# Loads over all partitions, and products of a zero block at the start, in a cross-attention and FFN kernel

## The chip, the cores and the metric

The kernel runs on one core of a Trainium2 chip, all in float32 (some operands in the fp32r form of it). The metric is the device time of one execution in microseconds, as the median of several runs. Beside these runs there is one profiled execution, from which all durations below are read.

## The reference

The input is x, 16 batches of 128 rows by 1024, and a context of the same shape. One layer of cross-attention is followed by a feed-forward product, each with a residual:

```python
x = x + xattn(layernorm(x), ctx, ctx, Wq, bq, Wk, bk, Wv, bv, Wo, bo)
x = x + ffn(layernorm(x), kernel, scale)
# xattn: Q = q @ Wq + bq (1024 -> 1024, 32 heads of 32)
#        K, V = ctx @ Wk + bk, ctx @ Wv + bv (1024 -> 256, 8 heads of 32; 4 query heads share one)
#        softmax(Q K^T / sqrt(32)) V per head, then @ Wo + bo
# ffn:   scale * concat(x[:819], -4 * x[819:]) @ kernel  (kernel: zeros and ones, 1024 x 1024)
```

## The kernel before

The batches go in groups of two (GB = 2), eight groups in all. For each group the kernel transposes the context, makes K and V, normalizes and transposes x, makes Q, runs the attention of each batch and head group, then the output projection and the feed-forward product. The large products (q, k, o, f) are done from the second group on in a form with seven half-size products in place of eight; sums of weight blocks that this needs are made early on (by GpSimd for Wq and Wo, in `combine`), stored in DRAM, and read again.

The order of the instructions is written out by hand. A `Stream` holds generators of matrix work in a queue, and events that fire at given times after a point ("later(us, fn)"). Every engine takes its instructions in the order in which this recording issues them. Thus a vector instruction that waits for a load also holds up what stands behind it on VectorE.

Weights come through a ring of eight tiles named `piece` (512 KB each, `fetch`, L243); the SP queue issues a new piece as soon as PE has released an old one. Nearly all transfers are issued on SP's queue (SPq in the profile), in order.

The context of a batch is loaded by `load_ctx` (L166) into a tile of 128 partitions x [4 blocks t][8 chunks c][32]. VectorE's 32x32 block transposes (`turn_ctx`, L445) then make the transposed context cT of it. For that the tile must have, on partition 32k + r, the rows 32t + r and the columns 256k to 256k + 255. Before the change each of the four DMAs of such a load fills one quarter of the partitions (fixed k, all t):

```python
src = key_value[b].rearrange("(t r) (k c f) -> k r t (c f)", r=32, k=NB, c=NC)
for k in range(NB):
    dst = c_t[k * 32 : (k + 1) * 32].rearrange("r t c f -> r t (c f)")
```

Wv and Wk are loaded once at the start in the same permuted order of rows, by `load_by_quadrants` (L175), as twelve and eight DMAs on three queues (ACT, GpSimd, SP). In the later groups normalized rows of x and of the input of the feed-forward product take the same way: `through_dram` stores a row tile in DRAM (L409) and reads it back in the block layout (L406, tiles `turn_x` and `turn_f`), for block transposes on VectorE (L471 and L983). The reading back must wait until the store has landed.

At the start the order is: context of batch 0, Wv, context of batch 1, Wk, then x of batches 0 and 1 (L183), the broadcast bias bo_b (L217), six pieces of Wq, the context of batches 2 and 3, two more pieces, eight half-size parts of Wo. PE starts with v for batch 0 and batch 1 (L418), then k, then the transposes of x (L434) and the products q of the first group.

Of the kernel before, what the change touches and what calls it, by code (L numbers as in the profile page):

```python
# [9 lines left out]
FP = mybir.dt.float32  # L10
# [8 lines left out]
P = 128  # L19
# [76 lines left out]
def kernel(  # L96
# [16 lines left out]
    nc = tc.nc  # L113
# [7 lines left out]
    NC = D // P  # L121
# [10 lines left out]
    const = ctx.enter_context(tc.tile_pool(name="const", bufs=1))  # L132
# [3 lines left out]
    ps_mm = ctx.enter_context(tc.tile_pool(name="ps_mm", bufs=2, space=PSUM))  # L136
# [6 lines left out]
    wk_sb = const.tile([P, NC, KV], FP, name="wk_sb")  # L143
    wv_sb = const.tile([P, NC, KV], FP, name="wv_sb")
# [13 lines left out]

    NB = P // 32

    def load_ctx(b, queues=(nc.sync,)):
        c_t = work.tile([P, NB, NC, 32], FP, tag="ctx", name=f"ctx{b}", bufs=2)
        src = key_value[b].rearrange("(t r) (k c f) -> k r t (c f)", r=32, k=NB, c=NC)
        for k in range(NB):
            dst = c_t[k * 32 : (k + 1) * 32].rearrange("r t c f -> r t (c f)")
            queues[k % len(queues)].dma_start(out=dst, in_=src[k])  # L166
        cs[b] = c_t

    def load_by_quadrants(dst, w, queues, *cuts):

        src = w.rearrange("(k c f) n -> k f c n", k=NB, f=32)
        n = 0
        for lo, hi in zip((0,) + cuts, cuts + (NC,)):
            for k in range(NB):
                queues[n % len(queues)].dma_start(  # L175
                    out=dst[k * 32 : (k + 1) * 32, lo:hi], in_=src[k][:, lo:hi]
                )
                n += 1

    def load_x(b, tag="row"):  # L180

        x_t = work.tile([P, D], FP, tag=tag, name=f"xn{b}", bufs=2)
        nc.sync.dma_start(out=x_t, in_=x[b])  # L183
        xns[b] = x_t
        if tag == "turn":
            turning.add(f"xn{b}")
# [11 lines left out]

    three = (nc.sync, nc.scalar, nc.gpsimd)
    load_ctx(0, three)
    load_by_quadrants(wv_sb, Wv, (nc.scalar, nc.gpsimd, nc.sync), 2, 4)
    load_ctx(1, three)
    load_by_quadrants(wk_sb, Wk, (nc.scalar, nc.gpsimd, nc.sync), 4)
    load_x(0)
    load_x(1)
    ident = const.tile([P, P], FP, name="ident")
    make_identity(nc, ident)
    minus_half = const.tile([P, 1], FP, name="minus_half")  # L210
# [183 lines left out]
    def through_dram(row, name, store, back, turn, then, tag="turn"):  # L394

        there = dram.tile([P, D], FP, name=f"dram_{name}")

        def load():
            bufs = 2 if tag == "turn" else TB
            c_t = work.tile([P, NB, NC, 32], FP, tag=tag, name=f"turn_{name}", bufs=bufs)  # L400
            if tag == "turn":
                turning.add(name)
            src = there.rearrange("(t r) (k n) -> k r t n", r=32, k=NB)
            for k in range(NB):
                dst = c_t[k * 32 : (k + 1) * 32].rearrange("r t c f -> r t (c f)")
                nc.sync.dma_start(out=dst, in_=src[k])  # L406
            stream.later(turn - back, lambda: then(c_t))

        stream.later(store, lambda: nc.sync.dma_start(out=there, in_=row) and None)  # L409
        stream.later(back, lambda: stream.when(lambda: tag != "turn" or len(turning) < 2, load))  # L410
# [718 lines left out]
    with tc.manual_schedule():  # L1129
# [17 lines left out]
        for j in range(GB):  # L1147
            load_ctx(GB + j)
# [83 lines left out]
        for grp in range(NGRP):  # L1232
# [39 lines left out]
            if not more:  # L1272
                for q in range(2 * NA):
                    b, a = grp * GB + q % GB, q // GB
                    start = stream.now
# [5 lines left out]
            for q in range(2 * NA):  # L1281
                b, a = grp * GB + q % GB, q // GB
                start = stream.now
# [64 lines left out]
```

## Time and profile before

| | |
|---|---|
| median of 3 runs | 770.59 us (770.08 to 770.86) |
| profiled execution, its own time | 765.46 us |
| span of the profile | 763.7 us |
| PE busy (TensorE's matrix instructions) | 746.6 us, 98% |
| DVE / ACT / POOL busy | 541.5 / 380.2 / 303.2 us |
| bytes moved by DMA | 203.36 MB, mean 266 GB/s |
| median time to landing, ctx loads on SP | 7.2 us, 128 KB each |
| median time to landing, turn_f and turn_x loads | 4.5 and 6.2 us, 128 KB each |

PE is TensorE's matrix instructions, PEld its weight loads, DVE VectorE, ACT ScalarE, POOL GpSimd; SPq is the queue of transfers that SyncE issues. Each float32 product shows as two matrix instructions in the profile. In rows of windows the columns are the window and its length, busy time of PE, PEld, DVE, ACT and POOL with the number of instructions, the granted clock of TensorE (1.00 is full), the mean busy share of the sixteen DMA engines and their rate in GB/s. An execution's own time is longer than its span by what lies around it, here 1.8 us.

### The profile page before, as it was taken

What the parts mean: (1) busy time and instruction counts of PE and PEld (TensorE: products, weight loads), DVE (VectorE), ACT (ScalarE), POOL (GpSimd) and SP (SyncE); (2) the same over time, 40 slices, a digit from 0 to 9 for tenths busy, and PEclk for the clock granted to TensorE, in tenths of its full rate; (3) what the DMA queues carried; (4) which work ended last, traced back from release to release, by engine and by line L of the source; (5) the groups of instructions that cost most, each with busy time, mean ns of one, the idle gap of its engine ahead of it and who ended that gap; (6) DMA issues with size and microseconds to landing.
All of it is one profiled execution on the core that took longest, in us unless ns stands there. A gap on an engine that the chain in (4) does not pass through costs nothing.

```text
span 763.7 us, 14898 instructions
## 1 busy us (share of the span) xinstructions
PE 746.6 (98%) x5232; PEld 563.4 (74%) x5232; DVE 541.5 (71%) x961; ACT 380.2 (50%) x1397; POOL 303.2 (40%) x356
## 2 busy tenths in 40 slices
PE   4999999999999999999999999999999999999997
PEld 3888884699747996489855998469984699546466
DVE  1456888977787667677676687865778766769586
ACT  0245764444735455344643447434464455568363
POOL 4069830342740146401652226322274113108582
PEclk9999999999999999999999999999999999999999
DMA  9989999989499895999779995899948988752912
GB/s 229 311 319 295 372 372 412 324 272 347 158 326 267 283 319 173 316 261 294 253 244 294 297 292 201 282 314 272 316 165 297 274 274 266 240 194 83 286 45 110
DMA packets 104314, 203.36 MB, mean 266 GB/s; under 512 B 8960, under 2 KB 58432, under 8 KB 104240
## 3 DMA queue, kind: packets, MB, share of 16 engines
q1 hardware_dynamic: 102480, 200.31, 81.8%
q10 hardware_dynamic: 1248, 1.11, 0.7%
q0 software_dynamic: 512, 0.99, 0.6%
q8 instruction: 41, 0.67, 0.4%
q14 instruction: 33, 0.27, 0.1%
HBM read 170.40 MB, written 31.98 MB: 265 GB/s over the span
## 4 chain that ended last, share of the span: by engine, by line
PE 90%; DVE 7%; DMA 2%; issue 1%; ACT 0%; SPq 0%; DVEq 0%
PE q_u L558 13%; PE o_u L862 12%; PE f_u L1017 7%; PE tpp L802 7%; PE q_v L558 7%; PE o_v L862 7%; PE k_u L558 5%; PE sc L769 4%; PE av L811 4%; PE q L418 4%; PE f_v L1017 3%; PE q_c L558 3%; PE k_v L558 3%; PE o_c L862 3%; PE f_c L1017 2%; PE k L418 2%
## 5 line engine op out<-in xcount | busy, mean ns | idle before, releaser
L785 ACT ACTIVATE p<-sc,negm 128x128 f32<-128x128 f32 x512 | 181.2, 370 | 147.3 <-DVE negm L781 73.1
L781 DVE TENSOR_REDUCE negm<-sc 128x4 f32<-128x512 f32 x128 | 86.9, 682 | 72.5 <-PE sc L769 72.5
L356 POOL CAST wide<-wf_sb 128x512 fp32r<-128x512 int8 x154 | 109.2, 749 | 64.0 <-PE f_u L1017 62.7
L804 ACT COPY pt<-tpp 128x512 f32<-128x512 f32 x128 | 75.1, 595 | 96.9 <-PE tpp L802 96.3
L797 DVE TENSOR_TENSOR p<-p,inv 128x512 f32<-128x512 f32 x128 | 103.4, 808 | 4.4
L785 ACT ACTIVATION_READ_ACCUMULATOR p<-sc,negm 128x1 f32 x512 | 106.3, 208 | 0.0
L196 POOL TENSOR_TENSOR x<-x,bo_b 128x256 f32<-128x256 f32 x64 | 50.3, 806 | 87.6 <-DMA x<-in_x_dram 74.9
L558 PE MATMUL q_u<-t,piece 128*128 128x128 f32 x672 | 81.3, 275 | 0.0
L558 PEld LDWEIGHTS q_u<-t,piece 128*128 128x128 f32 x672 | 78.1, 192 | 0.2 <-issue 0.2
L802 PE MATMUL tpp<-ident,p 128*128 128x128 f32 x512 | 75.9, 273 | 1.6 <-DVE p L797 1.6
L802 PEld LDWEIGHTS tpp<-ident,p 128*128 128x128 f32 x512 | 61.3, 141 | 20.1 <-issue 13.6
L862 PE MATMUL o_v<-piece,s 128*128 128x512 f32 x128 | 60.6, 601 | 0.2 <-DVE x L876 0.2
L862 PE MATMUL o_u<-piece,s 128*128 128x512 f32 x128 | 59.7, 597 | 0.5 <-DVE x L876 0.5
L862 PE MATMUL o_u<-piece,yT 128*128 128x512 f32 x128 | 58.6, 599 | 0.0
L819 ACT ACTIVATE yT<-av,bvT 128x512 f32<-128x512 f32 x32 | 22.0, 688 | 60.3 <-PE av L811 60.3
L769 PEld LDWEIGHTS sc<-kv,qT 32*128 32x128 f32 x1024 | 31.5, 186 | 25.7 <-issue 25.7
L374 POOL TENSOR_TENSOR rs_f<-ve_f,minus_half 128x1 f32<-128x1 f32 x16 | 9.5, 595 | 96.1 <-DVE ve_f L372 83.0
L961 POOL TENSOR_TENSOR s<-turn_f,turn_f 128x512 f32<-128x512 f32 x7 | 8.9, 1277 | 97.3 <-DVE turn_f L983 71.0
L354 ACT CAST wide<-wf_sb 128x512 fp32r<-128x512 int8 x70 | 43.2, 633 | 3.3 <-PE f_u L1017 3.0
L862 PEld LDWEIGHTS o_u<-piece,yT 128*128 128x128 f32 x128 | 23.5, 190 | 28.4 <-issue 26.7
L862 PEld LDWEIGHTS o_u<-piece,s 128*128 128x128 f32 x128 | 23.0, 190 | 27.6 <-issue 22.7
L862 PEld LDWEIGHTS o_v<-piece,s 128*128 128x128 f32 x128 | 22.4, 190 | 23.3 <-issue 18.9
(155 smaller groups left out, 1493.0 us busy)
## 6 DMA issues: line engine op xcount, KB each, us to landing
piece<-o SPq DMA_DIRECT2D x64, 512.0 KB, 4.8
piece<-q SPq DMA_DIRECT2D x56, 512.0 KB, 7.1
piece<-in_L_xattn_Wq_dram SPq DMA_DIRECT2D x50, 512.0 KB, 8.0
piece<-in_L_xattn_Wo_dram SPq DMA_DIRECT2D x48, 512.0 KB, 7.1
piece<-kv SPq DMA_DIRECT2D x18, 512.0 KB, 6.9
xn<-in_x_dram SPq DMA_DIRECT2D x16, 512.0 KB, 4.6
x<-in_x_dram SPq DMA_DIRECT2D x16, 512.0 KB, 5.1
ctx<-in_ctx_dram SPq DMA_DIRECT2D x60, 128.0 KB, 7.2
```

The source lines that it names most:

```text
L196: lambda cut=cut: nc.gpsimd.tensor_add(x_t[:, cut], x_t[:, cut], bo_b[:, cut]) and None,
L356: nc.gpsimd.tensor_copy(t, wf_sb[:, FFN[name], c])
L418: nc.tensor.matmul(mm, lhsT=lhsT, rhs=rhs, start=k == 0, stop=k == n - 1)
L558: nc.tensor.matmul(mm if part is None else mm[:, part], lhsT=lhsT, rhs=rhs, start=start and n == k == 0, stop=k == len(some) - 1, skip_gro ...
L769: nc.tensor.matmul(tiles[i][:, g], lhsT=qT[rows, g], rhs=kT[rows], start=True, stop=True,)
L781: nc.vector.tensor_reduce(negm, tile_, AX.X, ALU.max, negate=True)
L785: nc.scalar.activation(p[:, g], tile_[:, g], AF.Exp, bias=negm[:, g : g + 1], accum_out=total[:, g : g + 1],)
L797: nc.vector.tensor_mul(p, p, inv.unsqueeze(2).to_broadcast([P, NG, S]))
L802: nc.tensor.transpose(tp[:, g], p[:, g], ident)
L804: nc.scalar.copy(pt, tp)
L862: nc.tensor.matmul(mm, lhsT=lhsT[:, 2 * k + c], rhs=w[:, c], start=start and k == c == 0, stop=k == c == 1, skip_group_check=True,)
L1017: nc.tensor.matmul(mm, lhsT=part[:, c], rhs=w, start=start and c == n == 0, stop=c == HC - 1 and n == 1, skip_group_check=True,)
```

## The change

Three things change. First, each block load (context, and the readings back in `through_dram`) is cut the other way: each of its four DMAs now fills all 128 partitions for one t, with one packet of 1 KB per partition, as before 128 packets in all. Second, Wv and Wk are loaded with eight DMAs each, each over all partitions for one chunk c; the first loads are issued on two queues (SP and ACT) in place of three. Third, VectorE fills a 128x128 tile with zeros at the start, and TensorE multiplies it by itself nine times into a PSUM tile that nobody reads.

```diff
+    def blocks_in(dst, src, queues=(nc.sync,)):
+        src = src.rearrange("(t r) (k n) -> t k r n", r=32, k=NB)
+        for t in range(NB):
+            queues[t % len(queues)].dma_start(
+                out=dst[:, t].rearrange("p c f -> p (c f)"), in_=src[t]
+            )
+
     def load_ctx(b, queues=(nc.sync,)):
         c_t = work.tile([P, NB, NC, 32], FP, tag="ctx", name=f"ctx{b}", bufs=2)
-        src = key_value[b].rearrange("(t r) (k c f) -> k r t (c f)", r=32, k=NB, c=NC)
-        for k in range(NB):
-            dst = c_t[k * 32 : (k + 1) * 32].rearrange("r t c f -> r t (c f)")
-            queues[k % len(queues)].dma_start(out=dst, in_=src[k])
+        blocks_in(c_t, key_value[b], queues)
         cs[b] = c_t
 
-    def load_by_quadrants(dst, w, queues, *cuts):
-
-        src = w.rearrange("(k c f) n -> k f c n", k=NB, f=32)
...
+    def load_rows(dst, w, queues):
+
+        src = w.rearrange("(k c f) n -> c k f n", k=NB, f=32)
+        for c in range(NC):
+            queues[c % len(queues)].dma_start(
+                out=dst[:, c], in_=src[c]
+            )
...
-    three = (nc.sync, nc.scalar, nc.gpsimd)
-    load_ctx(0, three)
-    load_by_quadrants(wv_sb, Wv, (nc.scalar, nc.gpsimd, nc.sync), 2, 4)
-    load_ctx(1, three)
-    load_by_quadrants(wk_sb, Wk, (nc.scalar, nc.gpsimd, nc.sync), 4)
+    two = (nc.sync, nc.scalar)
+    load_ctx(0, two)
+    load_rows(wv_sb, Wv, two)
+    load_ctx(1, two)
+    load_rows(wk_sb, Wk, two)
     load_x(0)
     load_x(1)
+    blank = const.tile([P, P], FP, name="blank")
+    nc.vector.memset(blank, 0.0)
+    warm = ps_mm.tile([P, P], FP, tag="mm", name="warm")
+    for _ in range(9):
+        nc.tensor.matmul(warm, lhsT=blank, rhs=blank, start=True, stop=True)
...
-            src = there.rearrange("(t r) (k n) -> k r t n", r=32, k=NB)
-            for k in range(NB):
-                dst = c_t[k * 32 : (k + 1) * 32].rearrange("r t c f -> r t (c f)")
-                nc.sync.dma_start(out=dst, in_=src[k])
+            blocks_in(c_t, there)
             stream.later(turn - back, lambda: then(c_t))
```

Nothing else moves in the order of any engine's instructions.

More of the change, by code (lines that the diff above doesn't have):

```diff
@@ L159 @@
     NB = P // 32
+    def blocks_in(dst, src, queues=(nc.sync,)):
[4 more added lines that the diff above has]
+            )
     def load_ctx(b, queues=(nc.sync,)):
         c_t = work.tile([P, NB, NC, 32], FP, tag="ctx", name=f"ctx{b}", bufs=2)
-        src = key_value[b].rearrange("(t r) (k c f) -> k r t (c f)", r=32, k=NB, c=NC)
-        for k in range(NB):
-            dst = c_t[k * 32 : (k + 1) * 32].rearrange("r t c f -> r t (c f)")
-            queues[k % len(queues)].dma_start(out=dst, in_=src[k])
+        blocks_in(c_t, key_value[b], queues)
         cs[b] = c_t
-    def load_by_quadrants(dst, w, queues, *cuts):
-        src = w.rearrange("(k c f) n -> k f c n", k=NB, f=32)
-        n = 0
-        for lo, hi in zip((0,) + cuts, cuts + (NC,)):
-            for k in range(NB):
[L175 to L178, printed above, removed]
+    def load_rows(dst, w, queues):
[4 more added lines that the diff above has]
+            )
     def load_x(b, tag="row"):
@@ L402, in load @@
                 turning.add(name)
-            src = there.rearrange("(t r) (k n) -> k r t n", r=32, k=NB)
-            for k in range(NB):
-                dst = c_t[k * 32 : (k + 1) * 32].rearrange("r t c f -> r t (c f)")
-                nc.sync.dma_start(out=dst, in_=src[k])
+            blocks_in(c_t, there)
             stream.later(turn - back, lambda: then(c_t))
```

## The prediction

> **What bounds the kernel now.** I read the page first, then PE's waits, the chain of waits, the windows and the issue timeline.
>
> ```profile
> span 763.7 us, 14898 instructions
> PE 746.6 (98%) x5232; PEld 563.4 (74%) x5232; DVE 541.5 (71%) x961; ACT 380.2 (50%) x1397; POOL 303.2 (40%) x356
> ```
>
> TensorE is busy for all but 17.1 us of the span. Where the rest lies, the waits of PE say (us in total, times, longest):
>
> ```profile
> PE v L418 <- DMA wv_sb<-in_L_xattn_Wv_dram: 7.6, 2, 7.1
> PE v L418 <- DVE cT L445: 2.1, 1, 2.1
> PE tpp L802 <- DVE p L797: 1.6, 3, 0.8
> ```
>
> Only the first two concern loads: 9.7 us, all ahead of 15.88 us. After that PE never waits for a transfer. The chain of waits has the start in order of time (start, us):
>
> ```profile
> 2.12 5.02 DMA wv_sb<-in_L_xattn_Wv_dram
> 7.16 7.83 DMA ctx<-in_ctx_dram
> ...
> 15.88 3.72 PE v L418 x16
> 19.60 6.92 PE k L418 x32
> ```
>
> The windows give the rate of transfers in their last column, the DMA engines' share before it:
>
> ```profile
> 4.00:6.00 2.00, 0.00 (x0) 0.00 (x0) 0.03 (x1) 0.00 (x0) 1.82 (x4) 1.00 1.06 241
> 12.00:14.00 2.00, 1.79 (x8) 1.20 (x6) 0.00 (x0) 0.00 (x0) 0.00 (x0) 1.00 1.19 207
> 22.00:24.00 2.00, 2.00 (x11) 1.74 (x10) 1.49 (x3) 0.48 (x1) 0.48 (x1) 1.00 1.10 348
> 114.60:133.70 19.10, 19.10 (x83) 9.53 (x83) 16.75 (x34) 8.36 (x36) 1.20 (x2) 1.00 1.04 412
> ```
>
> Loads into 32 partitions (the first two rows) hold all engines busy, yet move 207 to 241 GB/s; transfers over 128 partitions, many with the same 1 KB packets, move 348, and 412 in the best stretch: 412/16 = 25.8 GB/s for one DMA engine. Last, one later group on SP's issue queue, and the vector transposes that use what it loaded:
>
> ```profile
> 419.53 8.24 SPq L166 DMA_DIRECT2D ctx<-in_ctx_dram  x8
> 430.66 0.38 SPq L409 DMA_DIRECT2D dram_f<-x2n  x1
> 437.41 2.62 SPq L406 DMA_DIRECT2D turn_f<-dram_f  x4
> 443.90 1.75 SPq L406 DMA_DIRECT2D turn_f<-dram_f  x4
> ```
> ```profile
> 452.48 1.31 DVE L983 STREAM_TRANSPOSE turn_f<-turn_f 128x512 f32<-128x512 f32 x2 [0.42 <-DMA turn_f<-dram_f]
> ```
>
> VectorE already waits 0.42 us for the second turn_f load: that transfer is just in time. It lands at about 452.4.
>
> **The changed loads.** Each load of a 512 KB block still is four DMAs of 128 KB, 128 packets of 1 KB. The destination gets 128 rows, but the source, written as (k r), has 4 as its outermost count and 32 inside it; before, both sides had 32 outermost, and every other bulk transfer 128. No row of before shows a transfer with fewer than 16 entries outermost, so its price is bounded from both sides. The good end is the 348 GB/s row: all engines at work, and every partition written. The bad end is that the engines are dealt out by the outermost count: 4 of 16, at worst the same four each time, so 4 x 25.8 = 103 GB/s. I take the bad end. The 32-row loads with a share of 1.06 to 1.19 show that 32 entries occupy all engines. Four entries cannot be dealt to sixteen engines without cutting them, and source and destination no longer have a common count of 16 or more in their first place. The nearest row for the speed of one engine is then the 412 row.
>
> The Trainium skill has a rule on this, on the page "DMA: Bandwidth & Descriptors", section "Why a DMA increments its semaphore by 16 and not by 1": a DMA gets the largest number of engines up to 16 that divides the slowest dimension of both patterns, and on the queues of SP and ACT these are the lowest-numbered. By it 128 and 4 give four engines, always the same; by the opposite case of 16 engines the sum would be rival B's. No row of before shows it.
>
> On those four engines a 128 KB block load puts 32 KB on each, and so does a 512 KB transfer over sixteen. At 25.8 GB/s either takes 1.27 us of them.
>
> *Start.* 24 loads x 1.27 = 30.5 us, begun at 2.1: the last of wk lands at 32.6. In the trace k ran from 19.4 with no wait. v for batch 1 needs ctx1, the 16th load (2.1 + 20.3 = 22.4), and hides in wk's landing. After the last wk come four instructions of k's first half (0.9) and its second half (3.46, half of 6.92): k ends at 37.0 rather than 26.5. The two xn loads queue behind wk on SP and land at 33.9 and 35.2; the normalization took 3.3 us for the first (20.05 to 23.33) and 3.1 for the second: 40.3. Then the transposes of x end near 42.6, where they ended at 28.6: **+14 us**.
>
> What is late next is the stream of transfers behind. bo_b and six pieces land by 44.0, ctx2 and ctx3 (8 x 1.27) by 54.2, two pieces and Wo's eight half-size parts by 61.8. In the trace GpSimd had the first of these parts at 41.2 and the rest by 43.9, so its sums start about 18 us later. It then is 96% busy (18.34 of 19.10 us) until 79, and the sums of Wq that it makes are stored, reloaded (issued 83.6 to 90.3) and used by PE from 89.4: nearly no slack. ctx4 and ctx5 add 8 x (1.27 - 0.60) = 5.4 us ahead of those stores (0.60 is 128 KB at 218 GB/s, a rate between the first two windows' rows). 18 + 5.4 is 23.4; with 1.6 us for the queue behind, **+25 us** by there, the 14 included. Bounds: 13, if the later stream is hidden, and 35, if an engine makes only 348/16 = 21.8 GB/s.
>
> *Each later group (91 us).* Between 419.5 and the use of the second turn_f stand 16 block loads and 8 other transfers: 24 x 1.27 = 30.5 us on the four engines. With the backlog at 419.5 (four transfers, 5 us) and 1.5 us to land: 456.5 rather than 452.4. If SP also drains while it waits for dram_f, the store that each turn_f load must follow (2 to 3 us, twice), it is 461. So VectorE stands still for 4 to 9 us; behind it in its queue are the maxima and the divisions of the softmax, and PE's transposes of p wait for these. Their slack (PE takes p at 358.7 that was divided by 353.3) covers some. I take 5 us for each of six groups: **+30 us**. Bounds: 0, and 11 where 65 transfers' worth (41 of 512 KB, 24 block loads) at 21.8 GB/s need 98 us rather than 91 and the wait for dram_f drains the queue as well.
>
> **The other edits.** GpSimd issues no first loads any more: its first block (about 5 us at 0.55 to 0.72 each) is off the path. ACT and SP issue twelve each at 0.31 to 0.45 us, less than the 1.27 us each takes to move; behind ACT's stands the table load (1.28 us), needed only by k's end. The memset costs about 0.22 us (the row of ident's) on a VectorE that first works at 5.97. Nine products are 18 instructions (each of v's 16 products shows as two of its 32); at twice the 111.6 ns spacing of 128x128 instructions (3.57/32) they take 4.0 us, about 1.2 to 5.2, and PE was idle until 7.13. If that cover were gone, they would cost at most those 4.0 us.
>
> What can they bring? v's first instruction took 767 ns and the next ones 634, with starts 0.43 us apart, against 379 and 0.216 later; the clock column shows 1.00 all through. Ten such starts are 2.1 us, and in before the wait for ctx1 (15.88) swallowed them. I take 0, with -2.1 as the other end where PE's first products set the pace.
>
> The skill's "TensorE: Matmul & The Clock Gate", Part 1, says that the array runs at half rate until some 3.4 us of activity and falls back after an idle window as long. The slow starts ended about 4.8 us after the first, near that. By it products that end at 5.2 ahead of a v later than 8.6 are forgotten: 0 again.
>
> **Sum.** 25 + 30 = 55 us. The profiled execution took 765.46 us (1.8 around the span), 5.1 under the median; added to the median of 770.59 this is 826 us.
>
> **Rivals.**
> - A, only the start suffers: four engines, but the slack in each group covers the delay. For it: SP waits mostly for PE to free pieces. Against: the 0.42 us row. 770.6 + 13 to 25 = 784 to 796.
> - B, faster: the loads run on all engines. 3 MB at 348 GB/s is 9.0 us rather than some 14 at 207 to 262, so ctx1 lands near 10 and v for batch 1 starts 4 to 5 us before 15.88; the products add up to 2.1. 764 to 767 us. It decides where the first loads move over about 262 GB/s, the most that a window of before's start shows. Against it: the outermost 4.
> - C, no difference: the loads get no faster, or what they gain is lost behind xn (20.05): 770.6 within 1.5 us.
>
> **How the numbers follow.** Forecast 0.57, A 0.25, B 0.15, C 0.03. Changes under 0.2% (1.5 us) are what a measurement here cannot tell from none. Slower 0.82, faster 0.15, same 0.03. The range takes A's low end with a small start, 776, and goes to 890, the high bounds (35 + 66 = 101, so 872) with some room for one engine slower than 21.8 GB/s; B and C stay outside.
>
> **What would show it.** Right: about 100 GB/s in the windows from 2 to 32 us, k ending near 37, later waits of DVE for turn_f by several us, and waits of PE for p or for pieces in each group. Wrong: 300 GB/s or more in the first windows with v for batch 1 before 12 us (B), or a late start followed by groups of 91 us (A).

## The result, and the profile after

The changed kernel takes 902.83 us (median of 6 runs, 899.81 to 906.37) against 769.76 us before (6 runs): the ratio is 1.1735, 95% interval 1.1701 to 1.1768. The profiled execution took 901.46 us, its span is 899.7 us, 136.0 us longer than the one before. The forecast was 826 us with a range up to 890: slower, as forecast, but by 133.1 us in place of 55.

The page of the changed kernel, first rows:

```profile
span 899.7 us, 14920 instructions
PE 787.7 (88%) x5250; PEld 591.5 (66%) x5250; DVE 543.5 (60%) x962; ACT 381.1 (42%) x1397; POOL 295.9 (33%) x347
```

PE's idle time grew from 17.1 to 112.0 us (899.7 - 787.7), that is by 94.9; its busy time grew by 41.1 us for 18 more instructions. The two make up the 136.0. The busy part is explained further down; the idle part is named by PE's waits (us in total, times, longest), of which the five largest are:

```profile
PE q_u L561 <- DMA piece<-q: 50.2, 10, 7.9
PE q_v L561 <- DMA piece<-q: 15.3, 8, 3.7
PE v L421 <- DVE cT L448: 12.8, 2, 7.5
PE o_v L865 <- DVE x L879: 8.7, 3, 4.9
PE k L421 <- DMA wk_sb<-in_L_xattn_Wk_dram: 4.9, 3, 3.8
```

Before, PE waited for loads at the start only. Now it waits 65.5 us for pieces of Wq, loads that the change does not touch: they queue behind the block loads. VectorE waits for the block loads themselves, and SP for the store that each turn_f must follow. First both lines as they were before, then after:

```profile
DVE turn_f L983 <- DMA turn_f<-dram_f: 6.3, 5, 2.9
...
SPq L406 <- DMA dram_f<-x2n: 45.5, 12, 7.1
```
```profile
DVE turn_f L986 <- DMA turn_f<-dram_f: 105.4, 14, 13.4
...
SPq L164 <- DMA dram_f<-x2n: 86.9, 13, 10.0
```

The windows at the start answer to those of before that showed a share of 1.06 to 1.19 (second to last column; the last is GB/s):

```profile
10.00:12.00 2.00, 0.00 (x0) 0.00 (x0) 0.07 (x1) 0.00 (x0) 0.00 (x0) 1.00 0.27 96
20.00:22.00 2.00, 2.00 (x4) 0.90 (x4) 0.00 (x0) 0.00 (x0) 0.00 (x0) 1.00 0.27 96
```

A share of 0.27 is about 4 of 16 engines. The windows from 10 to 30 us all read 0.27 and 96 or 97 GB/s; 96.5 GB/s / 4 = 24.1 GB/s for one engine, and a 128 KB load takes 131072 B / 96.5 GB/s = 1.36 us. The share stays there for 20 us with several loads under way on two queues, so all of them run on the same four engines. PE's timeline has the start (start, us, instructions, in brackets the idle time and who ended it):

```profile
43.73 6.05 PE L421 MATMUL k<-cT,wk_sb 128*128 128x256 f32 x18 [3.82 <-DMA wk_sb<-in_L_xattn_Wk_dram]
...
51.88 8.37 PE L421 MATMUL q<-xT,piece 128*128 128x256 f32 x38
```

q of the first group starts at 51.88 instead of 28.6. And one later group, SP's queue and then VectorE, at the place where the prediction showed it for before:

```profile
403.77 12.17 SPq L164 DMA_DIRECT2D ctx<-in_ctx_dram  x8
...
418.40 0.38 SPq L412 DMA_DIRECT2D dram_f<-x2n  x1
...
429.34 2.22 SPq L164 DMA_DIRECT2D turn_f<-dram_f  x4
431.66 0.46 SPq L412 DMA_DIRECT2D dram_f<-x2n  x1
432.22 1.17 SPq L249 DMA_DIRECT2D piece<-q  x2
439.54 2.21 SPq L164 DMA_DIRECT2D turn_f<-dram_f  x4
```
```profile
438.70 0.71 DVE L986 STREAM_TRANSPOSE turn_f<-turn_f 128x512 f32<-128x512 f32 x1 [11.93 <-DMA turn_f<-dram_f]
...
449.57 1.30 DVE L986 STREAM_TRANSPOSE turn_f<-turn_f 128x512 f32<-128x512 f32 x2 [5.79 <-DMA turn_f<-dram_f]
```

From the issue of a store of dram_f to the load that must follow it there are 10.9 us and 7.9 us; before, these gaps were 6.8 us (430.66 to 437.41) and 3.8 us (440.13 to 443.90). VectorE stands still 11.93 and 5.79 us for the two loads, where it stood 0.42 us before. Meanwhile the two pieces issued at 432.22 wait behind the block loads, and PE stands still too (PE's timeline):

```profile
440.89 2.90 PE L561 MATMUL q_u<-t,piece 128*128 128x128 f32 x12 [7.88 <-DMA piece<-q]
```

To split the loss by place, q_c, the first product of the halved form in each group, gives a clock that can be read in every run. In the summary of that tile (first and last start) its first instruction is at 85.2 us before and 112.9 after, its last at 626.5 and 750.9, and 137.2 and 148.8 us follow to the end. So the start costs 27.7, the six spans between 96.7 (16.1 each), and the end 11.6 us: 136.0.

### The profile page after: what moved, and what is told of

It is laid out like the page before. It is cut to its first block, busy times and chain, and to the rows that moved or that the text cites. A ratio compares the mean times of both kernels' runs of the same rounds, so it can differ in the third digit from the quotient of the medians.

```text
span 899.7 us, 14920 instructions
## 1 busy us (share of the span) xinstructions
PE 787.7 (88%) x5250; PEld 591.5 (66%) x5250; DVE 543.5 (60%) x962; ACT 381.1 (42%) x1397; POOL 295.9 (33%) x347
## 4 chain that ended last, share of the span: by engine, by line
PE 51%; DMA 30%; DVE 8%; SPq 7%; POOL 2%; issue 1%; DVEq 0%; ACT 0%; POOLq 0%
DMA dram_f<-x2n 12%; PE o_u L865 8%; SPq L164 6%; PE f_u L1020 6%; PE q_u L561 5%; PE o_v L865 5%; DMA piece<-q 5%; PE tpp L805 4%; PE q_v L561 4%; PE k_u L561 4%; PE sc L772 3%; PE av L814 3%; PE f_v L1020 3%; DMA turn_f<-dram_f 2%; DMA wv_sb<-in_L_xattn_Wv_dram 2%; PE k_v L561 2%
## 5 line engine op out<-in xcount | busy, mean ns | idle before, releaser
L561 PE MATMUL q_u<-t,piece 128*128 128x128 f32 x672 | 95.1, 301 | 50.2 <-DMA piece<-q 50.2
L561 PEld LDWEIGHTS q_u<-t,piece 128*128 128x128 f32 x672 | 90.5, 216 | 52.0 <-DVE inv L799 39.7
L805 PE MATMUL tpp<-ident,p 128*128 128x128 f32 x512 | 79.1, 281 | 4.3 <-DVE inv L799 2.5
L986 DVE STREAM_TRANSPOSE turn_f<-turn_f 128x512 f32<-128x512 f32 x28 | 19.1, 697 | 105.4 <-DMA turn_f<-dram_f 105.4
L805 PEld LDWEIGHTS tpp<-ident,p 128*128 128x128 f32 x512 | 63.8, 146 | 23.6 <-issue 16.4
L865 PE MATMUL o_v<-piece,s 128*128 128x512 f32 x128 | 62.9, 620 | 9.0 <-DVE x L879 8.7
L448 DVE STREAM_TRANSPOSE cT<-ctx 128x512 f32<-128x512 f32 x32 | 21.9, 693 | 43.5 <-DMA ctx<-in_ctx_dram 43.5
L561 PE MATMUL q_v<-xT,piece 128*128 128x128 f32 x224 | 31.7, 300 | 15.4 <-DMA piece<-q 13.6
```

The source lines that it names most:

```text
L561: nc.tensor.matmul(mm if part is None else mm[:, part], lhsT=lhsT, rhs=rhs, start=start and n == k == 0, stop=k == len(some) - 1, skip_gro ...
L805: nc.tensor.transpose(tp[:, g], p[:, g], ident)
L865: nc.tensor.matmul(mm, lhsT=lhsT[:, 2 * k + c], rhs=w[:, c], start=start and k == c == 0, stop=k == c == 1, skip_group_check=True,)
```

## The experiments

The ratios are to the kernel before, run beside each on the same chip; its medians there lie between 768.5 and 770.4 us. Most times below are medians of two runs (four for outer2, twelve for zeros_only, outer16, outer16_no_zeros and weights_wide).

**Which loads cost it.** Three parts of the change, each alone: `start_only` keeps the new first loads and the zero products and gives the later loads their old form, `later_only` the opposite, `zeros_only` keeps only the products.

```diff
 # start_only, load_ctx (and the old loop in through_dram)
-        blocks_in(c_t, key_value[b], queues)
+        if b < GB:
+            blocks_in(c_t, key_value[b], queues)
+        else:
+            ... # the four loads of before
 # later_only: the condition is b >= GB; through_dram as changed;
 # load_by_quadrants and the three queues of before; no zero products
```

> The first loads and the zero products as changed, all later block loads as before. Theory 1 (four engines, each part acts by itself): q of the first group starts near 52 us as in the changed kernel, and what is late there is still late at the end: 790 to 800 us. Theory 2 (the delay of the start alone sets off the later stalls, because the stream of transfers never catches up): over 850 us.

Measured 793.56 us, ratio 1.0302 (1.0263 to 1.0342): +23.1 us.

> The start as before, without the zero products; the later block loads (context from batch 2 on, turn_x, turn_f) as changed. Theory 1: the groups are 105 to 110 us long as in the changed kernel and the start is that of before: 865 to 885 us. Theory 2 (the start sets off the stalls): under 800 us.

Measured 880.26 us, ratio 1.1428 (1.1387 to 1.1469): +109.8 us. 23.1 + 109.8 = 132.9 us, and the whole change costs 902.83 - 769.76 = 133.1 us. The parts add up, and the later loads carry five sixths.

> The kernel before with the memset and the nine zero products alone. The wait for the context of batch 1 that ends at 15.9 us takes up whatever the first products gain: 770 us within 1. The rival, that a warm array shortens the start: 767 to 769 us.

Measured 769.83 us, ratio 1.0004 (0.9976 to 1.0031): nothing, in either direction. Its PE timeline shows why:

```profile
1.06 3.90 PE L212 MATMUL warm<-blank 128*128 128x128 f32 x18 [1.06 <-DVE blank L209]
7.16 3.11 PE L423 MATMUL v<-wv_sb,cT 128*128 128x256 f32 x8 [2.20 <-DMA wv_sb<-in_L_xattn_Wv_dram]
11.45 3.58 PE L423 MATMUL v<-wv_sb,cT 128*128 128x256 f32 x8 [1.18 <-DMA wv_sb<-in_L_xattn_Wv_dram]
```

The products, 18 instructions in 3.90 us, are over at 4.96, and v starts at 7.16 as it did at 7.13 before, still with about 0.4 us from one instruction to the next, twice the 0.216 us of full speed. The clock that the records grant between 10 and 14 us is 0.50. The sixteen instructions end at 15.03 us, where they ended at 13.79 before, so the slow part did not even become shorter; the wait for the second batch's cT swallows this as it did before.

**Is it the outermost count?** In these kernels only the way of cutting the source changes: 16, 8 or 2 entries outermost in place of 4. Each load still has 128 packets of 1 KB over all partitions. The rows then come in an order that the computation does not need, so these three kernels do not give the right output and serve for their times alone. With 16 entries:

```diff
-        src = src.rearrange("(t r) (k n) -> t k r n", r=32, k=NB)
+        src = src.rearrange("(b a) (t n) -> t a b n", a=16, t=NB)
...
-        src = w.rearrange("(k c f) n -> c k f n", k=NB, f=32)
+        src = w.rearrange("(b c a) n -> c a b n", a=16, c=NC)
```

> The changed kernel with the block loads and the loads of Wv and Wk read in another order of rows, whose source pattern has 8 entries outermost in place of 4; destination, packets of 1 KB, bytes and number of DMAs are the same (the order of the rows is not the one that the computation needs). Theory 1 (engines are dealt out by the outermost count): a DMA share near 0.5 and 190 to 200 GB/s in the first windows, 770 to 800 us. Theory 3 (the loss comes from loads over all partitions in so small packets, or from their issue): a share of 0.27 and about 900 us.

Measured 790.24 us, ratio 1.0259 (1.0204 to 1.0315).

> The same with 16 entries outermost. Theory 1: a DMA share near 1 and 300 GB/s or more in the first windows; v for batch 1 starts before 12 us, and the kernel is at or a little under the one before: 763 to 770 us. Theory 3: about 900 us.

Measured 767.47 us, ratio 0.9966 (0.9948 to 0.9983): 0.3% less than before, with 1 outside the interval.

> As outer8 and outer16, with 2 entries outermost in the source of every block and weight load (the rows do not come in the order that the computation needs; the transfers keep their size, 128 packets of 1 KB over all partitions). Theory 1 in its linear form (the engines are dealt out by the outermost count, one engine makes 24.1 GB/s, and a later group grows by all of the engine time that its 24 block loads take more than the 0.60 us each of before): 128 KB on two engines take 2.72 us, the share of the DMA engines in the start's windows is 0.13 to 0.15 at 48 GB/s, a group grows by 24 x (2.72 - 0.60) = 51 us (4 entries: 24 x (1.36 - 0.60) = 18.2 by the same sum, 16.5 measured), and the last first load lands some 35 us later than in the changed kernel: six groups 306, start about 60, so 1120 to 1190 us. Rival S (the group's growth is a queueing loss that saturates, some 16 us for any share of few engines): 900 to 960 us. Rival R (2 entries are dealt out otherwise than 4, for instance cut up): at or below the changed kernel's 903.

Measured 1156.99 us, ratio 1.5035 (1.4984 to 1.5086). One window of the start for each, with 8, 16 and 2 entries:

```profile
12.00:14.00 2.00, 2.00 (x6) 1.64 (x5) 0.00 (x0) 0.00 (x0) 0.00 (x0) 0.50 0.55 192
```
```profile
8.00:10.00 2.00, 2.00 (x6) 1.65 (x5) 0.00 (x0) 0.00 (x0) 0.00 (x0) 0.50 0.88 257
```
```profile
12.00:14.00 2.00, 0.00 (x0) 0.00 (x0) 0.00 (x0) 0.00 (x0) 0.00 (x0) 1.00 0.14 48
```

48, 96, 192 GB/s at shares of 0.14, 0.27, 0.55 for 2, 4, 8 entries: the engines are dealt out by the outermost count, and each moves 24 GB/s. With 16 entries the share is 0.88 and the rate 257 GB/s: no longer sixteen times 24, and under the 300 that were expected; what limits it there is not shown. The count of engines is the rule of the Trainium skill that the prediction weighed ("DMA: Bandwidth & Descriptors", "Why a DMA increments its semaphore by 16 and not by 1"), now shown here for 2, 4 and 8; which engines they are, no run here shows.

The same runs settle how a later group grows. If nothing hides them, its 24 block loads lengthen it by 24 x (time of one now - 0.60 us, the prediction's price of one before), the third column. The fourth is measured: the time between the first and the last q_c, six groups, less the 541.3 us of before, divided by six.

| entries outermost | us for 128 KB | 24 x (that - 0.60) | growth measured, us a group |
|---|---|---|---|
| 8 | 0.68 | 1.9 | 3.8 |
| 4 (the change) | 1.36 | 18.2 | 16.1 |
| 2 | 2.73 | 51.1 | 44.9 |

With 4 and 2 entries 88% of the added engine time arrives in the group. The 541.3 us are from one execution; zeros_only and outer16_no_zeros, which are no slower than before, have 547.7 and 546.6 us there, so a growth can be up to 1.1 us a group smaller (then 82 and 86%). The row of 8 is too small to test the sum. There is little slack, and the loss does not saturate.

**Which block loads.** The first loads as before and no zero products, and of the later loads one kind alone in the new form (shown against the changed kernel):

```diff
 # turn_f_only (turn_x_only: "x"; ctx_only: load_ctx for b >= GB instead)
-            blocks_in(c_t, there)
+            if name[0] == "f":
+                blocks_in(c_t, there)
+            else:
+                ... # the four loads of before
```

> The kernel before, with only the readings back of turn_f as changed (56 DMAs). Theory 1a (the later loss is VectorE's wait for turn_f, whose slack was 0): 40 to 70 us of the 110, so 810 to 840 us, with VectorE waiting for turn_f by 50 us or more. Theory 1b (it takes all three kinds of load together to overload the four engines): within 10 us of 770.

Measured 817.29 us, ratio 1.0611 (1.0562 to 1.0661): +47.8 us.

> The kernel before, with only the context loads from batch 2 on as changed (56 DMAs). Their uses lie 15 us behind, but on SP's queue they stand ahead of the store of dram_f. Theory 1a: 10 to 30 us, so 780 to 800, through a later dram_f and turn_f. Theory 1b: within 10 us of 770.

Measured 798.01 us, ratio 1.0361 (1.0311 to 1.041): +28.5 us.

> The kernel before, with only the readings back of turn_x as changed (48 DMAs). They are used 8 to 10 us after their issue. Theory 1a and 1b: within 10 us of 770.

Measured 795.69 us, ratio 1.0331 (1.0279 to 1.0383): +26.2 us, so the expectation that these would hide was wrong. 47.8 + 28.5 + 26.2 = 102.5 of the 109.8 us: again nearly additive. In each of the three, PE waits for pieces of Wq that it never waited for before, and VectorE waits for turn_f, also where turn_f itself has its old form. From ctx_only (all waits):

```profile
PE q_u L568 <- DMA piece<-q: 12.3, 5, 5.0
...
DVE turn_f L993 <- DMA turn_f<-dram_f: 27.3, 10, 4.6
```

So each kind costs by itself, and loads that are not slow themselves come late behind it. The kinds do not cost the same. Eight loads a group add 8 x (1.36 - 0.60) = 6.1 us of engine time; read from q_c as above, a group grows by 6.7 us for turn_f (40.5 in six), 5.4 for turn_x (32.3) and 4.4 for ctx (26.3). They sum to 16.5 us, where the whole change has 16.1; each can be up to 1.1 us smaller, as above.

**Is SP's wait for the store the loss?** It had risen from 45.5 to 86.9 us, and while SP waits, no piece is issued behind it. `late_f` takes this wait away, by reading back 8 us later:

```diff
-    FBACK = ((7.0, 18.0), (8.0, 19.0))
+    FBACK = ((15.0, 26.0), (16.0, 27.0))
```

> The changed kernel, with the reading back of turn_f and its transposes recorded 8 us later, so that on SP's queue six pieces of Wq and its sums stand ahead of the reading back in place of one, and less is queued behind the store of dram_f. Theory W (the groups lose to SP standing in wait for dram_f, 86.9 us in all, with the pieces of q behind it): groups of 95 to 102 us in place of 107.7, so 835 to 875 us, with PE's wait for pieces of q well under 65 us. Theory E (the four engines themselves are full: 65 transfers of 1.35 us are 88 us a group): 890 us or more.

Measured 926.14 us, ratio 1.2046 (1.1989 to 1.2104), slower than the change itself. Most of the wait is gone, the loss is not (waits of VectorE, of SP and of PE):

```profile
DVE turn_f L986 <- DMA turn_f<-dram_f: 91.8, 12, 9.2
...
SPq L164 <- DMA dram_f<-x2n: 16.3, 5, 4.0
...
PE q_v L561 <- DMA piece<-q: 24.0, 9, 4.4
```

PE's waits for pieces of q halve (24.0 and 8.7 for q_u, together 32.7 instead of 65.5 us), but VectorE still waits 91.8 us for turn_f, and the feed-forward product, whose operands these are, now comes later. So turn_f is late without SP's long wait too. That the wait costs nothing is not shown, since PE's waits fell with it and the edit moves other work too. The waits of turn_x_only say more: there SP waits hardly longer for the store than the 45.5 us of before, and 26.2 us are lost all the same.

```profile
SPq L416 <- DMA dram_f<-x2n: 50.0, 13, 8.0
```

**Does the second queue slow the first?** At the start the last chunk of Wk was used at 43.73, 11 us later than forecast (32.6). ACT's queue carries half of Wk in 1 KB packets, while SP's already sends x, bo_b and pieces of Wq with packets of 4 KB over the same engines. `one_queue` puts all 24 first loads on SP, ahead of these.

```diff
-    two = (nc.sync, nc.scalar)
+    two = (nc.sync,)
```

> The changed kernel, with all 24 first loads on SP's queue in place of SP and ACT by turns. Theory Q (the last chunks of Wk land as late as 43.7 us since their 1 KB packets on ACT's queue take turns with the 4 KB packets of x, bo_b and the pieces on SP's): the last chunk lands near 34 us, q of the first group starts at 44 to 47 us in place of 51.9, 895 to 899 us in all. Theory not Q (the four engines just need that long): 51 us or later.

Measured 905.01 us, ratio 1.1772 (1.1719 to 1.1824), as the change itself. PE's timeline:

```profile
39.99 5.84 PE L421 MATMUL k<-cT,wk_sb 128*128 128x256 f32 x18 [1.36 <-DMA wk_sb<-in_L_xattn_Wk_dram]
```

The last chunk came 3.7 us earlier, where 9 to 10 were expected, and q at 49.4 instead of 51.9. So issuing on two queues accounts for about a third of the 11 us, and nothing of it reached the end.

**What is left of the idea.** `outer16_no_zeros` is outer16 without the zero products; `weights_wide` is the kernel before with Wk and Wv loaded over all partitions in five DMAs on two queues, after their rows were put in that order ahead of the launch.

```diff
 # weights_wide
+    def load_rows(dst, w, queues, *cuts):
+        src = w.rearrange("(p c) n -> p c n", p=P)
+        for n, (lo, hi) in enumerate(zip((0,) + cuts, cuts + (NC,))):
+            queues[n % len(queues)].dma_start(out=dst[:, lo:hi], in_=src[:, lo:hi])
```

> The kernel with 16 entries outermost (the order of the rows is not the one that the computation needs), without the memset and the zero products. If the products warm the array for v: 1 to 2 us slower than outer16 (0.9966 of before), so 0.998 to 0.999. If they do nothing: the same ratio within 0.2%.

Measured 766.67 us, ratio 0.9973 (0.9953 to 0.9993). Against 0.9966 with the products, that is no difference; what little outer16 wins comes from the loads.

> The kernel before, with the rows of Wk and Wv put in the order of the partitions ahead of the launch (as Wq's columns already are), so that each partition reads one contiguous run and five DMAs over 128 partitions with 128 entries outermost take the place of twenty; nothing else changed. 2 MB at about 350 GB/s in place of 230 are 2.9 us less: v for batch 1 starts 2 to 4 us earlier and the kernel takes 766 to 768 us, 0.995 to 0.997 of before. Rival: the start is bound by x's normalization (20.05 us), and nothing is gained.

Measured 768.29 us, ratio 0.9988 (0.9969 to 1.0008). v for the second batch starts at 14.97 instead of 15.88, less than the 2 to 4 us expected, and q of the first group at 27.69 instead of 28.6; the whole time is not clear of no change.

## Why the prediction was right in kind and wrong in size

- **Four engines.** Right. The bad end of the bounds held: 0.27 of the engines, 96.5 GB/s where 103 was taken from the 412 row (24.1 and not 25.8 GB/s for one engine, 1.36 and not 1.27 us). This difference of 7% runs through every term but explains little.
- **The start, +25 us.** Right in sum by luck: an underestimate and an overestimate cancel. By q of the first group 14 us were forecast and 23.3 came. PE waited for each chunk of Wv on the way, and Wk's last chunk came at 43.73: the first loads move only 52 to 83 GB/s from 2 to 10 us, and two queues cost 3.7 us more than one. Of the further 11 us that were forecast behind it only 4.4 came (27.7 at the first q_c). start_only's +23.1 us agrees.
- **"5 us for each of six groups: +30 us".** This is the step that failed: 16.1 us a group were measured, over its upper bound of 11, which is 96.7 us in six, and 11.6 more behind the last q_c, where the last group's f has its loads too and the sum had nothing. The prediction set 24 transfers (30.5 us; 16 of them block loads) against a window of some 33 us, for one stall of VectorE, and let the slack of the softmax cover some of that. The runs show instead that the group grows by 82 to 88% of the added engine time of all its 24 block loads. The cover did not exist, because the block loads share their engines with the pieces of Wq. By the prediction's own count of 65 transfers a group, each now 1.36 us on the four engines, these have 88 us of work in a group that was some 90 us long (541.3 / 6), so almost nothing is left to catch up in. A ring that looked comfortable (PE waited 0 us for a piece of q before) emptied, since each piece, as the prediction has it, also puts a sixteenth of its bytes on each of the four slow engines, behind the block loads.
- **The wait for the store.** Forecast as 2 to 3 us, twice a group. It was 3.8 us a time before already (45.5 us in 12) and is 6.7 after (86.9 in 13). late_f shows that turn_f is late without it; how much of the 16.1 us it carries stays open.
- **The clock, a term that the sum did not have.** Of the 136.0 us, 41.1 are PE being busy for longer. After a stall PE works slowly, as the windows around the wait at 440 show (clock granted in the third column from the end):

```profile
434.00:437.00 3.00, 0.00 (x0) 0.00 (x0) 0.00 (x0) 0.00 (x0) 0.00 (x0) 0.95 0.67 228
437.00:440.00 3.00, 0.00 (x0) 0.00 (x0) 1.30 (x3) 0.55 (x2) 0.00 (x0) 0.50 0.65 204
443.00:446.00 3.00, 3.00 (x16) 3.00 (x16) 0.78 (x2) 0.58 (x1) 0.00 (x0) 0.50 0.84 233
```

  After the wait that ends at 440.89 PE works at half the clock. Taken over the whole trace, busy time times (1 - granted clock) comes to some 24 us, and to 0.0 before. That is more than half of the 41.1; 4.2 more are the zero products, and 5.1 the products v at the start (22.7 in place of 17.6 us, at a clock that reads 1.00). What makes up the last 8 is not shown. An idle PE is thus paid for twice, once as the stall and once as the slow work that follows. The Trainium skill's "TensorE: Matmul & The Clock Gate", Part 1, would have given this term, had the prediction applied it to the later stalls and not only to the zero products.
- **Zero products and the rest at nothing.** The zero products: right, 1.0004 (0.9976 to 1.0031). Of the other small terms one was off: ACT and SP were to issue a first load in 0.31 to 0.45 us, and SP took 8.19 us for its four of Wv, 2 us each. Whether this slows the start or only shows that the four engines are full is not shown.

```profile
2.27 8.19 SPq L177 DMA_DIRECT2D wv_sb<-in_L_xattn_Wv_dram  x4
```

- **The rivals.** A (only the start) is refuted by later_only. B's condition, more than 262 GB/s at the start, is met by outer16 in some windows, and its time (767.47 us) lies just above B's 764 to 767; the change itself stays outside it because of the outermost 4.

## What to carry to other kernels

Before a load is cut anew, look at the outermost count of the source as well as at the partitions of the destination: 128 partitions do not help if the other side begins with 4. Where all bulk transfers share the engines, cost a slower one at its full added engine time, times its number in a period, unless the trace shows those engines idle in that period (here 82 to 88% of it came, all kinds together); that PE waits for no transfer now says nothing of slack. And if a stall of several us on PE is forecast, add the work that follows at half the clock.

## What the runs showed of the hardware that was not expected

- One DMA engine moves 24 GB/s with 1 KB packets, and the rate is proportional to the outermost count: 48, 96, 192 GB/s for 2, 4, 8. With 16 it is 257 to 264 GB/s in the windows between 6 and 10 us.
- Products of zeros that end 2.2 us before the real work did not bring it to full speed, though a pause of 2.2 us is shorter than the 3.4 us that the prediction reckoned with: the first sixteen instructions of v ended at 15.03 us with them and at 13.79 without. In before's record the clock reads 1.00 while the first instructions of v are at half speed; in the record with the products it reads 0.50 from 8 to 14 us. Whether the products had reached full speed by their end is not shown.
- With half of the first loads on ACT's queue, beside SP's with its packets of 4 KB, the last chunk of Wk came 3.7 us later than with all on one queue. That the size of the packets is the reason was argued and not shown.
